# VectorE's queue in a neighbourhood-quantile stage: from the planner's order to one written out by hand

## The chip, the cores and the metric

The kernel runs on one core of a Trainium2 chip. The metric is the device time in microseconds (us) of one launch, as the median of several runs. Each engine of a core (TensorE, VectorE, ScalarE, GpSimd, SyncE; in the profile PE, DVE, ACT, POOL, SP) works through a queue of its own in order. An instruction that waits for a semaphore holds up all that stand behind it on its engine.

## The reference

Sixteen graphs of 1024 nodes with 64 channels go through four layers, each followed by a residual sum and a layer norm. Layers 0, 1 and 3 are a normalised propagation, a gated 8-head attention and a plain propagation. Layer 2 is the one that matters here. Its core is this:

```python
nd = adj_d > 0                                   # some neighbours are thinned out first
s = jnp.sort(jnp.where(nd[..., None], x[:, None, :, :], jnp.inf), axis=2)
nv = nd.sum(2)
for tau, w in zip((0.25, 0.5, 0.75), (0.25, 0.5, 0.25)):
    pos = tau * jnp.maximum(nv - 1, 0)
    lo, hi = floor(pos), ceil(pos)
    agg = agg + w * (v_lo + (pos - lo) * (v_hi - v_lo))   # v_lo = s[..., lo, :], v_hi = s[..., hi, :]
```

For every node and channel it takes three quantiles over the node's neighbours, each interpolated between two order statistics. A two-layer network follows.

## The kernel before

The kernel handles two graphs at a time, in eight passes. A pass has layer 0, then attention (during which the sorting network for the previous pair runs on VectorE), then the quantile stage of the previous pair (`quantiles`). Layers 2 and 3 of a pair end one pass later.

No neighbour list is sorted in the quantile stage. Each channel's 1024 values were sorted once over all nodes, and a node's neighbour set is a bit pattern over the sorted order: 32 words of 32 bits. The stage finds the word that holds the wanted order statistic, takes that word out, finds the bit in it, and looks the value up:

- `words` makes E, 0/1 and power-of-two matrices, on VectorE (an "E-word", two instructions of 128x1024). `half_word` multiplies E with the neighbour matrix on TensorE (one magic matmul and eight of 128x512), and ScalarE evicts the result into V (three 16-bit planes: a running count and the two halves of the word).
- A *step* is one (group of four channels, quantile) pair. 16 groups x 3 quantiles x 2 graphs give 96 steps; eight steps make a *unit*, so there are twelve units.
- `compare` (L900, VectorE, 128x2048) compares the running counts with the limits: `lt`. `one_hot` takes differences of neighbouring rows by four matmuls with `dif`, and ScalarE casts them into `oh`, which marks the word.
- `pick` (L918, VectorE, two instructions of 128x3072) multiplies V by the one-hots: `m`, two buffers. `sum_words` (12 small matmuls, `tonesb`) adds the rows up into `wps`, one PSUM tile per unit.
- After the eighth step of a unit, `kth_bit` searches all of the unit's words for the bit: one ScalarE cast of wps to `wb`, then about fifty short VectorE instructions on 16-bit integers, in five parts between `yield`s, giving `r2` and `r64`.
- `distances` (12 matmuls with `pen`, 16 with `bd`), `least_values` (4) and `sum_values` (8, f32) then look the value up, one earlier step (`look`) at a time, and the last of a unit multiplies by the weights and writes the result out (L983, L984).

The PSUM banks of `bank` are four, shared by half words, one-hots and distances.

Who orders what: TensorE's instructions in the stage go through `product`, which ties each to the one before it, so their order is that of the program. All other engines are ordered by the framework's planner, which puts an instruction that it expects to be ready ahead of one that it expects to wait. In program order a step is: pick (two products), compare for the next step, distances, half of the half words, least values, one-hot of the next step, sum of values, the other half words, `sum_words`, a part of the search in steps 0 to 3, and new E-words in steps 4 to 7. `MORE` says how many half words a step has. Lookups trail the products by 8 + `PARTS` = 12 steps. After step 96 a tail does the last twelve lookups.

Of the kernel before, what the change touches and what calls it, by code (L numbers as in the profile page):

```python
# [25 lines left out]
P = 128  # L26
# [8 lines left out]
OFF = 8192.0  # L35
OFF0 = 128.0
# [6 lines left out]
PARTS = 4  # L43
LAG = PARTS + 1
MORE = (1, 3, 3, 3, 1, 0, 0, 0)
# [75 lines left out]
def gnn_kernel(ctx: ExitStack, tc: tile.TileContext, a: dict, out: bass.AP):  # L121
# [558 lines left out]
    def rank_limits(gr, qe, qn):  # L680
# [14 lines left out]
        def limits(q):  # L695

            lim = gr.lim[q] = qe.tile([P, 2, N], U16, name="lim", bufs=LB)
            nc.scalar.activation(lim[:, 0], cnt, AF.Copy, scale=0.25 * (q + 1), bias=-0.25 * (q + 1) - 0.375)
            for s in (1, 0):
                nc.vector.tensor_scalar(lim[:, s], lim[:, 0], 32.0, OFF0 + 32.0 * (s + 1), op0=ALU.mult, op1=ALU.add)  # L700

# [21 lines left out]
    def kth_bit(pool, wps, kd, r2, r64):  # L723


        sh = [P, 512]
        v = nc.vector

        def u16(name, shape=sh):
            return pool.tile(shape, U16, name=name)  # L730

        wb = pool.tile([P, NW, 512], BF, name="wb")
        nc.scalar.copy(wb, wps)
        yield
        X = wb.bitcast(U16)
        v.tensor_scalar(X[:, 0], X[:, 0], OFF0, None, op0=ALU.subtract)
        v.tensor_scalar(X[:, 1:3], X[:, 1:3], OFF, None, op0=ALU.subtract)
        k = u16("k")
        S = u16("S", [P, 2, 512])
        U = u16("U", [P, 2, 512])  # L740
        a, c = U[:, 0], S[:, 0]
        v.tensor_scalar(a, X[:, 0], 5, None, op0=ALU.logical_shift_right)
        v.tensor_tensor(k, kd, a, ALU.subtract)
        v.tensor_scalar(X[:, 0], X[:, 0], 31, None, op0=ALU.bitwise_and)

        def counts(x, s1, s2, s4, t):

            v.tensor_scalar(t, x, 1, 0x5555, op0=ALU.logical_shift_right, op1=ALU.bitwise_and)
            v.tensor_tensor(s1, x, t, ALU.subtract)
            v.tensor_scalar(t, s1, 2, 0x3333, op0=ALU.logical_shift_right, op1=ALU.bitwise_and)  # L750
            v.tensor_scalar(s2, s1, 0x3333, None, op0=ALU.bitwise_and)
            v.tensor_tensor(s2, s2, t, ALU.add)
            v.tensor_scalar(t, s2, 4, None, op0=ALU.logical_shift_right)
            v.tensor_tensor(s4, s2, t, ALU.add)
            v.tensor_scalar(s4, s4, 0x0F0F, None, op0=ALU.bitwise_and)

        counts(X[:, 0:2], S, S, S, U)
        yield
        v.tensor_scalar(U, S, 8, None, op0=ALU.logical_shift_right)
        v.tensor_tensor(S, S, U, ALU.add)  # L760
        v.tensor_scalar(S, S, 0x1F, None, op0=ALU.bitwise_and)

        M = u16("M", [P, 2, 512])
        v.tensor_tensor(a, S[:, 0], S[:, 1], ALU.add)
        v.tensor_tensor(M[:, 0], S[:, 0], k, ALU.is_le)
        v.tensor_tensor(M[:, 1], a, k, ALU.is_le)
        v.tensor_tensor(S, S, M, ALU.mult)
        v.tensor_tensor(k, k, S[:, 0], ALU.subtract)
        v.tensor_tensor(k, k, S[:, 1], ALU.subtract)
        v.copy_predicated(X[:, 0], M[:, 0], X[:, 1])  # L770
        v.copy_predicated(X[:, 0], M[:, 1], X[:, 2])
        pos = u16("pos")
        v.tensor_scalar(pos, M[:, 0], 5.0, None, op0=ALU.mult)
        v.tensor_scalar(a, M[:, 1], 14.0, None, op0=ALU.mult)
        v.tensor_tensor(pos, pos, a, ALU.add)
        yield

        counts(X[:, 0], X[:, 1], X[:, 2], c, a)
        for width, z, mask in ((8, None, 15), (4, 2, 15), (2, 1, 3), (1, 0, 1)):
            v.tensor_scalar(c, c if z is None else X[:, z], mask, None, op0=ALU.bitwise_and)  # L780
            v.tensor_tensor(a, c, k, ALU.is_le)
            if width > 1:
                v.tensor_tensor(c, c, a, ALU.mult)
                v.tensor_tensor(k, k, c, ALU.subtract)
                v.tensor_scalar(a, a, float(width), None, op0=ALU.mult)
                n = {8: 3, 4: 2, 2: 1}[width]
                v.tensor_tensor(X[:, 0:n], X[:, 0:n], a[:, None, :].to_broadcast([P, n, 512]),  # L787
                                ALU.logical_shift_right)
            v.tensor_tensor(pos, pos, a, ALU.add)
            if width == 8:  # L790
                yield
        v.tensor_scalar(r64, pos, 64.0, None, op0=ALU.mult)
        searched[:] = [v.tensor_tensor(r2, pos, pos, ALU.mult)]  # L793

    def words(pool, g, w, rk, u_w, b_w):
# [12 lines left out]
        if w == 0:  # L808
            d = Ev.bitcast(F16)
            nc.vector.tensor_tensor(d, over_j(tk_c), over_t(u_w), ALU.subtract)  # L810
            nc.vector.tensor_scalar(Ev, d, 0.0, 2048.0, op0=ALU.max, op1=ALU.min)
        else:
            nc.vector.tensor_tensor(Ev, over_t(rk), over_j(t_c), ALU.is_equal)
            nc.vector.tensor_tensor(Ev, Ev, over_t(b_w), ALU.mult)
        return E

    def quantiles(ip, rk, u_w, b_w):
# [12 lines left out]
        with ExitStack() as es:  # L830

            kb, qe, qn = [es.enter_context(tc.tile_pool(name=name, bufs=1, reuse_waits="tile"))
                          for name in ("kb", "qe", "qn")]
# [43 lines left out]
            def half_word(gr, g, w, hf, matmul):  # L877
# [10 lines left out]
                if w == 0:  # L888
                    nc.scalar.activation(gr.V[g][:, 0, cols], ps, AF.Copy, scale=2.0 ** -6,  # L889
                                         bias=OFF0 - MAGIC[0] / 64 - 63 / 128)  # L890
# [6 lines left out]
            def compare(u, s):  # L897
                gr, g, q = u.pairs[s]
                u.lt = qe.tile([P, 2, N], BF, name="lt", bufs=LTB)
                nc.vector.tensor_tensor(u.lt, gr.V[g][:, None, 0, :].to_broadcast([P, 2, N]), gr.lim[q], ALU.is_lt)  # L900

            def one_hot(u, s):
                oh = qn.tile([P, 2, N], F16, name="oh", bufs=U8N + LAG)
                for kk in range(2):
                    for hf in range(2):
                        cols = slice(hf * 512, (hf + 1) * 512)
                        ps = bank([P, 512])
                        product(ps, dif, u.lt[:, kk, cols], start=True, stop=True)
# [3 lines left out]
            def pick(u, s):  # L912
                gr, g, q = u.pairs[s]
                u.m = [None, None]
                nonlocal picked
                for kk in range(2):
                    u.m[kk] = qe.tile([P, NW, N], BF, name="m", bufs=2)
                    picked = nc.vector.tensor_tensor(u.m[kk], gr.V[g].bitcast(BF),  # L918
                                            u.oh[s][:, kk, None, :].to_broadcast([P, NW, N]), ALU.mult)

            def sum_words(u, s):
                if s == 0:
                    u.wps = psw.tile([P, NW, 512], F32, name="wps")
                for w in range(NW):
                    for t in (1, 3, 0, 2):
                        hf, kk = t // 2, t % 2
                        product(u.wps[32 * t:32 * t + 32, w, :], tonesb[:, s, :],
                                u.m[kk][:, w, hf * 512:(hf + 1) * 512],
# [5 lines left out]
            def distances(u, s, spare=False):  # L934
# [13 lines left out]
                if spare:  # L948
                    for h in range(2):
                        x = qn.tile([P, 2, N], F16, name="oh", bufs=U8N + LAG)  # L950
# [21 lines left out]
            def sum_values(u, s):  # L972
# [4 lines left out]
                if s == U8N - 1:  # L977
                    res = qn.tile([P, 512], F32, name="vals", bufs=5)
                    if u is units[-1]:
                        nc.scalar.copy(res, u.acc)  # L980
                        nc.gpsimd.tensor_tensor(res, res, gr.cf[u.n % 3], ALU.mult)
                    else:
                        nc.vector.tensor_tensor(res, u.acc, gr.cf[u.n % 3], ALU.mult)  # L983
                    nc.gpsimd.dma_start(agg_d[gr.bb][:, u.n, :], res)  # L984
# [4 lines left out]
            units = [SimpleNamespace(n=i // U8N % NU, pairs=pairs[i:i + U8N], oh=[], vals={}) for i in range(0, len(pairs), U8N)]  # L989
# [6 lines left out]
            def elements():  # L996
# [4 lines left out]
                gr.E.setdefault(g, []).append(words(qe, gr.bb * G + g, w, rk, u_w, b_w))  # L1001
                made += 1

            def more_elements():
                while todo and made + 1 <= used // 2 + EB:
                    elements()

            def more_words(n, matmul=product):
                nonlocal used
                for k, w, hf in islice(halves, n):  # L1010
                    while len(groups[k][0].E.get(groups[k][1], [])) <= w:
                        elements()
# [4 lines left out]
            with tc.high_priority():  # L1017
                while made < 2 * EW:
                    elements()
            more_words(2 * EW, nc.tensor.matmul)  # L1020
            more_elements()
# [7 lines left out]
            compare(*steps[0])  # L1029
            one_hot(*steps[0])  # L1030
# [3 lines left out]
            search = None  # L1034
            for i, (u, s) in enumerate(steps):
# [17 lines left out]
                pick(u, s)  # L1053
                if i + 1 < len(steps):
                    compare(*steps[i + 1])
                if look:
                    distances(*look)
                more_words(more // 2)
                if look:
                    least_values(*look)  # L1060
                if i + 1 < len(steps):
                    one_hot(*steps[i + 1])
                if look:
                    sum_values(*look)
                more_words(more - more // 2)
                sum_words(u, s)
                if s < PARTS and search is not None:
                    next(search, None)
                if s >= PARTS or i < U8N:
                    more_elements()  # L1070
                if s == U8N - 1:
                    u.r2 = qn.tile([P, 512], F16, name="r2", bufs=2)
                    u.r64 = qn.tile([P, 512], F16, name="r64", bufs=2)
                    search = kth_bit(kb, u.wps, u.pairs[0][0].kc[u.n % 3], u.r2, u.r64)
                    next(search)
            before = None
            for i, look in enumerate(steps[-U8N - PARTS:]):
                if i < PARTS:
                    next(search, None)
                if before and i == PARTS:  # L1080
                    sum_values(*before)
                    before = None
                distances(*look, spare=i % 2 == 1)
# [4 lines left out]
            sum_values(*before)  # L1088

# [255 lines left out]
```

## Time and profile before

| | us |
|---|---|
| median of 3 runs (12822.29 to 12823.69) | 12823.57 |
| the profiled execution | 12824.17 |
| its span, first to last instruction | 12822.4 |
| VectorE busy, whole span | 10529.5 |
| TensorE busy, whole span | 11097.9 |
| ScalarE busy, whole span | 7375.6 |
| products L918, 1536 of 1753 ns | 2636.8 |
| compares L900, 768 of 1220 ns | 936.8 |

A group's row gives the busy time, the mean of one in ns, the idle time of its engine just ahead of it, and what ended that. A matmul's end is modelled, so TensorE's busy share is an upper bound of its work; what it could do is better read from distances between starts.

From the timeline, the first product of the first stage starts at 1262.4 and the last one ends at 2110.6: 848.2 us for 96 steps. From first product to first product the twelve units of that stage take 56.0, 76.7, 70.1, 75.0, 75.4, 74.7, 70.3, 70.2, 71.2, 70.3, 70.2 and 68.3 us. The tail's last lookup ends 60.9 us after the last product. The other seven stages agree with this within 2.5 us in each unit.

### The profile page before, as it was taken

Reading aid. Unit: us, or ns where it says so; the run is one execution under the profiler, and the core shown is the slowest. Engines: PE = TensorE matmul, PEld = TensorE weight load, DVE = VectorE, ACT = ScalarE, POOL = GpSimd, SP = SyncE. Lnnn points to the kernel's source line nnn. Section 1 sums busy time; section 2 is a strip of 40 time slices with the busy share of each in tenths; the row PEclk is TensorE's granted clock in tenths of the full one; section 3 lists DMA queues with packets and bytes.
Section 4 is the critical chain, followed back from the end, with each engine's and each line's share of the span. In section 5 each row is a group of like instructions: output and inputs, shape, how many; then the busy total and the mean of one; then the engine's idle time right before and its main releaser. Section 6 shows DMA issues by size and latency. Waiting matters only on the chain.

```text
span 12822.4 us, 208955 instructions
## 1 busy us (share of the span) xinstructions
PE 11097.9 (87%) x82560; PEld 4623.9 (36%) x82560; DVE 10529.5 (82%) x18662; ACT 7375.6 (58%) x13684; POOL 547.1 (4%) x836
## 2 busy tenths in 40 slices
PE   7989897998979899798997989879898798983897
PEld 3545222552225422254222532235322353221222
DVE  3587898788977889788996889968898788988895
ACT  4656565565646566465664656646566465651564
POOL 0000000000000000000000000000000000000000
PEclk8989998999989999899998999989899899996998
DMA  2021002200031000310003100031000410002001
GB/s 81 31 90 39 4 5 97 65 26 4 6 103 62 23 5 5 121 46 20 5 6 125 44 18 5 6 128 42 16 5 6 135 44 8 8 14 88 4 5 47
DMA packets 352246, 510.07 MB, mean 40 GB/s; under 512 B 120480, under 2 KB 275488, under 8 KB 349216
## 3 DMA queue, kind: packets, MB, share of 16 engines
q1 hardware_dynamic: 288656, 367.77, 8.8%
q10 hardware_dynamic: 33040, 86.88, 2.0%
q0 software_dynamic: 29568, 42.05, 1.1%
q8 instruction: 649, 10.63, 0.3%
q14 instruction: 333, 2.73, 0.1%
HBM read 380.08 MB, written 116.46 MB: 39 GB/s over the span
## 4 chain that ended last, share of the span: by engine, by line
PE 49%; DVE 25%; ACT 13%; issue 4%; DMA 4%; SPq 0%; ACTq 0%; DVEq 0%
PE bank L875 18%; ACT vals L961 7%; PE banks L536 6%; PE bank L558 5%; PE bank L572 5%; DVE m L918 5%; PE acc L875 4%; PE wps L875 2%; DVE key L1184 2%; PE bank L412 2%; DMA at<-in_adjT 2%; PE banks L387 1%; DVE lt L900 1%; DVE s L543 1%; DVE wb L787 1%
## 5 line engine op out<-in xcount | busy, mean ns | idle before, releaser
L918 DVE TENSOR_TENSOR m<-V,oh 128x3072 bf16<-128x3072 bf16 x1536 | 2636.8, 1753 | 274.8 <-PE wps L875 228.1
L961 ACT ACTIVATE vals<-bank 128x512 f32<-128x512 f32 x2880 | 1488.1, 602 | 1382.2 <-PE bank L875 1381.1
L875 PE MATMUL bank<-ndT,E 128*128 128x512 fp8e4 x7936 | 1914.9, 385 | 0.0
L543 DVE CUSTOM_DVE_ANT_0 s<-banks,adj 128x1024 f32<-128x1024 f32 x1024 | 1214.8, 1221 | 643.9 <-PE banks L536 639.6
L909 ACT CAST oh<-bank 128x512 f16<-128x512 f32 x3072 | 1595.2, 632 | 94.3 <-PE bank L875 94.1
L875 PE MATMUL bank<-lt,dif 128*128 128x512 bf16 x3072 | 1073.5, 393 | 319.7 <-DVE lt L900 73.1
L562 ACT COPY pT<-bank 128x512 f32<-128x512 f32 x1536 | 802.4, 594 | 815.3 <-PE bank L558 815.3
L551 ACT ACTIVATE s<-s,mx 128x1024 f32<-128x1024 f32 x1024 | 1176.4, 1160 | 73.6 <-DVE mx L543 71.0
L536 PE MATMUL banks<-kT,qT 64*128 64x512 f32 x4096 | 1115.3, 626 | 63.6 <-DVE mx L543 40.6
L900 DVE TENSOR_TENSOR lt<-V,lim 128x2048 bf16<-128x2048 uint16 x768 | 936.8, 1220 | 228.6 <-PE bank L875 228.3
L875 PEld LDWEIGHTS <-E 128*128 128x128 bf16 x7936 | 701.6, 98 | 1055.8 <-issue 367.8
L558 PEld LDWEIGHTS bank<-ident,s 128*128 128x128 f32 x8192 | 897.1, 142 | 405.5 <-issue 288.7
L558 PE MATMUL bank<-ident,s 128*128 128x128 f32 x8192 | 1028.9, 280 | 0.0
L572 PE MATMUL bank<-pT,v 128*64 128x256 f32 x8192 | 1007.8, 389 | 0.0
L875 PE MATMUL bank<-r,pen 32*128 32x512 f16 x5856 | 614.0, 391 | 418.4 <-DVE r L793 368.5
L875 PE MATMUL bank<-oh,bd 64*64 64x512 f16 x11712 | 818.5, 393 | 0.0
L875 PE MATMUL acc<-vals,bonesf 128*32 128x512 f32 x5760 | 794.3, 616 | 0.0
L875 PE MATMUL wps<-m,tonesb 128*32 128x512 bf16 x9216 | 656.2, 387 | 71.7 <-DVE m L918 71.7
L889 ACT ACTIVATE V<-bank 128x512 uint16<-128x512 f32 x512 | 305.6, 597 | 657.7 <-PE bank L875 601.4
L893 ACT ACTIVATE V<-bank 128x512 uint16<-128x512 f32 x512 | 306.0, 598 | 641.6 <-PE bank L875 631.3
L572 PEld LDWEIGHTS bank<-pT,v 128*64 128x64 f32 x8192 | 548.5, 138 | 313.9 <-issue 50.9
L1184 DVE TENSOR_TENSOR key<-key 128x512 f32<-128x512 f32 x880 | 579.2, 688 | 26.4 <-DMA key<-x2T_d 25.5
(274 smaller groups left out, 14426.5 us busy)
## 6 DMA issues: line engine op xcount, KB each, us to landing
at<-in_adjT SPq DMA_DIRECT2D x256, 512.0 KB, 5.6
masks_d<-mask SPq DMA_DIRECT2D x440, 128.0 KB, 1.7
mask<-masks_d SPq DMA_DIRECT2D x440, 128.0 KB, 2.1
adj<-in_adj SPq DMA_DIRECT2D x96, 512.0 KB, 5.3
ad<-in_adj ACTq DMA_DIRECT2D x64, 512.0 KB, 6.2
agg_d<-vals POOLq DMA_DIRECT2D x96, 256.0 KB, 2.3
agg<-agg_d ACTq DMA_DIRECT2D x16, 1536.0 KB, 8.6
nd_d<-nd SPq DMA_DIRECT2D x128, 128.0 KB, 1.9
```

The source lines that it names most:

```text
L536: then(nc.tensor.matmul(ss[h][:, hf * 512:(hf + 1) * 512], gr.qk[hp, 0][HALF[h], k * P:(k + 1) * P], gr.qk[hp, 1][HALF[h], hf * 512:(hf + ...
L543: last = nc.vector.tensor_tensor_reduce(s, ss[h], gr.adj[k], -1.0, 3.0e38, ALU.add, ALU.min, mx)
L551: then_act(nc.scalar.activation(s, s, AF.Exp, bias=mx, scale=-1.0, accum_out=sm))
L558: then(nc.tensor.transpose(ps[:, m, :], exps[h][0][:, (4 * mh + m) * P:(4 * mh + m + 1) * P], ident))
L562: then_act(nc.scalar.copy(dst, ps))
L572: then(nc.tensor.matmul(po[HALF[h]], gr.v[:, 4 * mh + m, (2 * hp + h) * C:(2 * hp + h + 1) * C], pT[h][mh][:, m, :], start=(mh == 0 and m ...
L875: then(nc.tensor.matmul(*args, **kw))
L900: nc.vector.tensor_tensor(u.lt, gr.V[g][:, None, 0, :].to_broadcast([P, 2, N]), gr.lim[q], ALU.is_lt)
L909: nc.scalar.copy(oh[:, kk, cols], ps)
L918: picked = nc.vector.tensor_tensor(u.m[kk], gr.V[g].bitcast(BF), u.oh[s][:, kk, None, :].to_broadcast([P, NW, N]), ALU.mult)
L961: nc.scalar.activation(vals[t], ys[t], AF.Relu)
L1184: i = v.tensor_tensor(*args)
```

## The change

- VectorE's instructions of the stage that go through a new helper `InOrder` (products, compares, E-words, the search, the result's multiply) are tied to each other in program order, as TensorE's are.
- The search is cut into 27 *runs*, and its instructions are rearranged so that a run ends where the next instruction needs the last one's result. `RUNS` says how many runs a step has, in six steps instead of four. They alternate with the large instructions of the step: product, run, (result, run,) product, run, compare, run, halves of E-words and runs.
- Compares and one-hots are made two steps ahead, and two of each are made before the loop. `lt` and `m` move to a pool of their own; their buffer counts stay 1 and 2.
- In TensorE's order the least values come right after the distances, then one half word, the one-hot, a further half word where `MORE` is 2, the sum of values, `sum_words`.
- The offsets of the three planes of V become equal (256), so one ScalarE pass removes them from `wb` instead of two VectorE subtractions. Some masks in the bit counts are left out or moved.
- `PARTS` is 6: lookups trail by 14 steps. The result's multiply and its DMA come one step later. At most `AT_ONCE` E-words are made in a step.

```diff
+RUNS = (5, 4, 2, 8, 3, 5)
+PARTS = len(RUNS)
+AT_ONCE = (1, 1, 0, 1, 0, 1, 2, 2)
+MORE = (1, 2, 1, 2, 1, 2, 1, 1)
-PARTS = 4
-MORE = (1, 3, 3, 3, 1, 0, 0, 0)
...
+    class InOrder:
+        def __init__(self):
+            self.then = in_sequence()
+        def __getattr__(self, name):
+            def op(*args, **kw):
+                i = getattr(nc.vector, name)(*args, **kw)
+                self.then(i)
+                return i
+            return op
...
         nc.scalar.copy(wb, wps)
+        nc.scalar.activation(X, X, AF.Copy, bias=-OFF)
         yield
-        X = wb.bitcast(U16)
-        v.tensor_scalar(X[:, 0], X[:, 0], OFF0, None, op0=ALU.subtract)
-        v.tensor_scalar(X[:, 1:3], X[:, 1:3], OFF, None, op0=ALU.subtract)
         v.tensor_scalar(a, X[:, 0], 5, None, op0=ALU.logical_shift_right)
+        v.tensor_scalar(X[:, 0], X[:, 0], 31, None, op0=ALU.bitwise_and)
         v.tensor_tensor(k, kd, a, ALU.subtract)
-        v.tensor_scalar(X[:, 0], X[:, 0], 31, None, op0=ALU.bitwise_and)
...
+        def nibbles(x, s1, s2, s4, t):
             v.tensor_scalar(t, x, 1, 0x5555, op0=ALU.logical_shift_right, op1=ALU.bitwise_and)
+            yield
             v.tensor_tensor(s1, x, t, ALU.subtract)
+            yield
             v.tensor_scalar(t, s1, 2, 0x3333, op0=ALU.logical_shift_right, op1=ALU.bitwise_and)
             v.tensor_scalar(s2, s1, 0x3333, None, op0=ALU.bitwise_and)
+            yield
             v.tensor_tensor(s2, s2, t, ALU.add)
+            yield
             v.tensor_scalar(t, s2, 4, None, op0=ALU.logical_shift_right)
+            yield
             v.tensor_tensor(s4, s2, t, ALU.add)
-            v.tensor_scalar(s4, s4, 0x0F0F, None, op0=ALU.bitwise_and)
+            yield
+        yield from nibbles(X[:, 0:2], S, S, S, U)
+        v.tensor_scalar(U, S, 8, 15, op0=ALU.logical_shift_right, op1=ALU.bitwise_and)
+        v.tensor_scalar(S, S, 15, None, op0=ALU.bitwise_and)
+        yield
         v.tensor_tensor(S, S, U, ALU.add)
-        v.tensor_scalar(S, S, 0x1F, None, op0=ALU.bitwise_and)
+        yield
         v.tensor_tensor(a, S[:, 0], S[:, 1], ALU.add)
         v.tensor_tensor(M[:, 0], S[:, 0], k, ALU.is_le)
         v.tensor_tensor(M[:, 1], a, k, ALU.is_le)
+        yield
+        v.copy_predicated(X[:, 0], M[:, 0], X[:, 1])
         v.tensor_tensor(S, S, M, ALU.mult)
+        v.tensor_scalar(pos, M[:, 0], 5.0, None, op0=ALU.mult)
         v.tensor_tensor(k, k, S[:, 0], ALU.subtract)
+        yield
+        v.tensor_scalar(a, M[:, 1], 14.0, None, op0=ALU.mult)
         v.tensor_tensor(k, k, S[:, 1], ALU.subtract)
         v.copy_predicated(X[:, 0], M[:, 1], X[:, 2])
         v.tensor_tensor(pos, pos, a, ALU.add)
+        yield from nibbles(X[:, 0], X[:, 1], X[:, 2], c, a)
+        v.tensor_scalar(c, c, 15, None, op0=ALU.bitwise_and)
+        for width, z, mask in ((8, 2, 15), (4, 1, 3), (2, 0, 1)):
+            yield
             v.tensor_tensor(a, c, k, ALU.is_le)
+            yield
+            v.tensor_tensor(c, c, a, ALU.mult)
+            v.tensor_scalar(a, a, float(width), None, op0=ALU.mult)
+            v.tensor_tensor(k, k, c, ALU.subtract)
+            n = z + 1
+            v.tensor_tensor(X[:, 0:n], X[:, 0:n], a[:, None, :].to_broadcast([P, n, 512]),
+                            ALU.logical_shift_right)
             if width == 8:
                 yield
+            v.tensor_tensor(pos, pos, a, ALU.add)
+            v.tensor_scalar(c, X[:, z], mask, None, op0=ALU.bitwise_and)
+        yield
+        v.tensor_tensor(a, c, k, ALU.is_le)
+        yield
+        v.tensor_tensor(pos, pos, a, ALU.add)
+        yield
         v.tensor_scalar(r64, pos, 64.0, None, op0=ALU.mult)
         searched[:] = [v.tensor_tensor(r2, pos, pos, ALU.mult)]
...
-                u.lt = qe.tile([P, 2, N], BF, name="lt", bufs=LTB)
+                u.lt[s] = qm.tile([P, 2, N], BF, name="lt", bufs=LTB)
...
-                oh = qn.tile([P, 2, N], F16, name="oh", bufs=U8N + LAG)
+                oh = qn.tile([P, 2, N], F16, name="oh", bufs=U8N + PARTS + 2)
...
-            compare(*steps[0])
-            one_hot(*steps[0])
+            for st in steps[0:2]:
+                compare(*st)
+                one_hot(*st)
...
-                pick(u, s)
-                if i + 1 < len(steps):
-                    compare(*steps[i + 1])
+                def large():
+                    pick(u, s, 0)
+                    yield
+                    if results:
+                        result()
+                        yield
+                    pick(u, s, 1)
+                    yield
+                    if i + 2 < len(steps):
+                        compare(*steps[i + 2])
+                        yield
+                    yield from more_elements(AT_ONCE[s] if i >= U8N else 2)
+                for _ in zip_longest(large(), islice(search, RUNS[s] if s < PARTS else 0)):
+                    pass
                 if look:
                     distances(*look)
+                    least_values(*look)
+                more_words((more + 1) // 2)
+                if i + 2 < len(steps):
+                    one_hot(*steps[i + 2])
                 more_words(more // 2)
                 if look:
-                    least_values(*look)
-                if i + 1 < len(steps):
-                    one_hot(*steps[i + 1])
-                if look:
                     sum_values(*look)
-                more_words(more - more // 2)
                 sum_words(u, s)
-                if s < PARTS and search is not None:
-                    next(search, None)
-                if s >= PARTS or i < U8N:
-                    more_elements()
```

## Prediction

> **What bounds the kernel now.** I read the page first, then the stage windows. The quantile stage runs eight times, some 910 us each, so it is over half of the span.
>
> ```profile
> PE 11097.9 (87%) x82560; PEld 4623.9 (36%) x82560; DVE 10529.5 (82%) x18662; ACT 7375.6 (58%) x13684; POOL 547.1 (4%) x836
> ```
>
> In the windows (PE, PEld, DVE, ACT and POOL busy) the first row is one stage, the second one unit of eight steps inside it:
>
> ```profile
> 1235.00:2145.00 910.00, 794.58 (x6296) 250.11 (x6300) 817.86 (x1231) 547.10 (x1036) 47.98 (x86) 0.95 0.03 9
> 1760.50:1830.70 70.20, 66.71 (x551) 20.91 (x547) 66.18 (x100) 45.39 (x88) 4.85 (x9) 1.00 0.02 6
> ```
>
> TensorE and VectorE are both 95% busy in a unit, so neither can be late without the unit growing. The list of waits shows how they hold each other, over all eight stages (us, times, longest):
>
> ```profile
> PE bank L875 <- DVE r L793: 368.5, 56, 18.3
> ...
> DVE lt L900 <- PE bank L875: 228.3, 255, 5.9
> DVE m L918 <- PE wps L875: 228.1, 304, 2.9
> ```
>
> The timeline of the end of a unit, with no search in it, shows one step in full:
>
> ```profile
> 1748.45 0.83 PE L875 MATMUL wps<-m,tonesb 128*32 128x512 bf16 x12
> 1749.22 0.61 PE L875 MATMUL bank<-r,pen 32*128 32x512 f16 x8
> 1749.38 3.43 DVE L918 TENSOR_TENSOR m<-V,oh 128x3072 bf16<-128x3072 bf16 x2 [0.47 <-PE wps L875]
> ...
> 1751.36 1.84 PE L875 MATMUL bank<-lt,dif 128*128 128x512 bf16 x4
> ...
> 1753.13 1.06 PE L875 MATMUL acc<-vals,bonesf 128*32 128x512 f32 x8
> 1753.24 1.23 DVE L900 TENSOR_TENSOR lt<-V,lim 128x2048 bf16<-128x2048 uint16 x1 [0.43 <-PE bank L875]
> 1754.02 0.83 PE L875 MATMUL wps<-m,tonesb 128*32 128x512 bf16 x12
> ```
>
> Two things matter. The products (m, L918) wait until the sums (wps) of the step before have read the only two m buffers: the sums end at 1749.28, the products start at 1749.38. And the planner put the compare for one-hot j+1 ahead of the products of step j, so its one-hot (1751.36) had lt long before, and only the products stood before the sums. TensorE's queue is full: 5.56 us per step (1748.45 to 1754.02) plus 2.14 for each half word (1740.35 to 1742.49), 10.67 of them per unit: 8 x 5.56 + 10.67 x 2.14 = 67.3, of 70.3.
>
> **What the change does to this loop.** TensorE's written order in step i is now: lookup, half word, one-hot i+2, perhaps another half word, sum of values, sums i. VectorE's is: product, run, product, run, compare i+2, and the rest. So the one-hot needs the compare that stands *behind* this step's products, the sums stand behind the one-hot in one queue, and the next products need the sums. That is a closed loop through both engines. What is queued behind the waiting product on VectorE is everything: its order is fixed, so search and E-words cannot pass. The old waits on lt and m go; this one is next late. Step by step:
>
> - Two products start 1.68 apart (3.43 - 1.75) and the compare takes 1.22: 2 x 1.68 + 1.22 = 4.58.
> - The runs between them. An instruction followed by an independent one costs its duration less some 0.09: 128x512 scalar ops 0.20, tensor ops 0.34; 128x1024 0.34 and 0.60; predicated copies 0.60; shifts 0.87, 0.61 and 0.34. The two runs ahead of the compare come, for s = 0 to 5, to 1.68, 1.28, 3.42, 0.74, 0.88, 2.10; in s = 6 the result multiply (0.68, L983) costs 0.61; in s = 7 nothing. Together 10.7.
> - From the compare's end: 0.06 to the one-hot; four one-hot matmuls 1.07 with free banks (1295.54 to 1296.61), 1.20 behind a half word (1715.27 to 1716.47), 1.77 as above, waiting for banks; I take 1.15, since a half word now gives the banks time; 0.88 (1753.13 to 1754.02, sum of values), 0.83 (sums), 0.09 to the product: 3.01. A half word behind the one-hot makes it 5.15, in s = 1, 3, 5 (s = 3 in two units of three).
> - VectorE's work behind the compare hides inside this: 0 us in s = 2, 2.0 in s = 4, 2 to 3 elsewhere. Only in s = 3 is it about 4.7 (runs of 0.34, 0.20, 0.34, 0.20, 0.34 and 1.75, 0.4 for dependent neighbours, an E-word of 1.1), above the 3.01 of every third unit.
> - TensorE's work in front of the one-hot (1.74 + 0.40 + 2.14 = 4.3) lies beside products and compare, and so sets nothing.
> - First run of a unit: wps goes through a ScalarE cast (1.44, L733) and now a second ScalarE pass in place of two VectorE subtractions (0.29 + 0.42). No row shows it; its nearest are 1.05 (128x1024, L698) and the cast's 1.44 on as many elements. I take 1.44. The run is ready 3.1 us after the sums, the product ahead of it ends after 1.84: 1.3 of wait in s = 0 (0 if ScalarE is quicker, 4 if four evictions go between).
>
> So the steps are 10.6, 11.0, 11.0, 10.3, 8.5, 11.8, 8.2, 7.6: **79.0 us per unit**, where today's are 70.3 (units 2 and 6 to 10) and 75 (3 to 5, which also prepare the second graph).
>
> **What is saved** lies beside this loop. VectorE loses the two subtractions and two masks (0.42 + 0.29; a third only changes place): 1.4 us a unit. Neighbours that depend on each other are split:
>
> ```profile
> 1719.17 0.43 DVE L781 TENSOR_TENSOR U<-S,k 128x512 uint16<-128x512 uint16 x1
> 1719.63 0.42 DVE L783 TENSOR_TENSOR S<-S,U 128x512 uint16<-128x512 uint16 x1
> 1720.09 0.43 DVE L784 TENSOR_TENSOR k<-k,S 128x512 uint16<-128x512 uint16 x1
> 1720.43 0.29 DVE L785 TENSOR_SCALAR U<-U 128x512 uint16<-128x512 uint16 x1
> ```
>
> Dependent ones start 0.03 after the last ended, independent ones 0.09 before: 0.12 a pair, some 30 pairs, 3.6 us a unit. VectorE's own work would then be near 62 us of 79, so none of it reaches the end. [...]
>
> **The sum**, per stage. Units 2 to 10: 9 x 79.0 = 711, plus half of the 14 us of second-graph work (the rest falls into the new waits): 718 against 647, +71. Unit 0 has neither lookup nor search: 8 x (4.58 + 2.13) + 3 x 2.14 = 60.1 against 56.0, +4. Unit 1 has no lookup until s = 6, so no sum of values: 79.0 - 6 x 0.88 + 0.5 (s = 3 is then set by VectorE's 4.7) = 74.2 against 76.8, -3, as its 18.3 us wait for the first search goes: lookups now trail by 14 steps, not 12. Unit 11 runs out of half words after s = 1 and has no compare in the last two steps (9.0 in s = 3, 9.7 in s = 5, 5.0 and 3.4 at the end): 68 against 68, 0. Tail: the two extra lookups fill the 12.2 us that TensorE waits there for the last search; -2. The result DMA moves one step later past POOL's bd loads; nobody reads it before the stage ends, so 0. Together +71, times 8 = +567. The profiled execution took 12824.17 (span 12822.4); with the median of 12823.57 it comes to 12,824 + 567 = **13,390 us**.
>
> **Rivals.**
> 1. *Faster.* The loop is slack, because the work behind each compare covers TensorE's answer. It decides where that work exceeds 3.0 (5.2) us in every step. TensorE alone would then set the unit: 67.3 less 8 x 0.6 of bank waits = 62.4, with some loss 66. 9 units save 4.2 each, the second graph's 14 us and 9 of unit 1 go: -61 x 8, about 12,340. For it: the runs are nearly equal, 2.9 to 3.9 us a step. Against it: 10.7 of their 20 us stand ahead of the compare, and s = 2 keeps none behind it. 0.12.
> 2. *No difference.* The loop binds but at 70 us: it would need the answer in 1.9 instead of 3.0, which the rows exclude, or a VectorE order in which only neighbours through the new helper are tied and the planner still lifts compares. About 12,820. 0.02.
> 3. *Slower still.* The first run waits 4 us, not 1.3, and one-hots stay at 1.77: 2.7 + 5.0 per unit, +77 a stage, near 14,000; half of it, 13,700. TensorE also slows after long idling (r,pen 1.04 instead of 0.61 after the 18.3 us wait); I assume 1 to 3 us do not. 0.16.
> 4. *My forecast*, +42 (no first-run wait, one-hot 1.07, second graph free) to +100 a stage (a third of case 3's +77 more): 13,160 to 13,620. 0.70.
>
> Range 13,050 to 13,760: cases 4 and half of 3, with the low end stretched towards 1. A measurement tells 0.2% (26 us) from no change: faster 0.12, same 0.02, slower 0.86.
>
> **What would show it.** Right: products waiting on wps with over 1,000 us in the waits; one-hots waiting on lt in nearly every step; lt no longer waiting on the bank; VectorE and TensorE each near 62 to 66 us of a 79 us unit; step s = 2 near 11 us with nothing between compare and product; r waits short. Wrong: a unit at or under 70 us, or VectorE over 90% busy in it.

## The result, and the profile after

The changed kernel takes **13,796.67 us** (median of 4 runs, 13,784.33 to 13,805.12) beside 12,822.93 for the kernel before (12,809.88 to 12,823.69): 1.076 times as long, interval 1.0743 to 1.0780. I had said 13,390 and a range of 13,050 to 13,760. The direction and the loop are as predicted; 975 us were lost (span 12,822.4 to 13,797.8) where I had 567.

The page's first part, of after:

```profile
PE 11133.8 (81%) x82560; PEld 4686.0 (34%) x82560; DVE 10347.7 (75%) x18278; ACT 7564.9 (55%) x13780; POOL 541.8 (4%) x836
```

VectorE has 182 us less to do, TensorE about what it had, and both now stand still more. In the windows (PE, PEld, DVE, ACT and POOL busy, then the granted clock) the first row is one stage, the second one unit of eight steps:

```profile
1263.00:2230.00 967.00, 752.23 (x5913) 240.28 (x5913) 747.23 (x1078) 535.36 (x988) 39.88 (x74) 0.92 0.02 4
1861.00:1943.00 82.00, 66.19 (x551) 21.47 (x547) 65.30 (x97) 47.44 (x88) 4.84 (x9) 0.94 0.02 5
```

The unit of 70.2 us has become one of 82.0, with the same 66 us of TensorE and 65 of VectorE in it. The list of waits (us, times, longest) says what fills the rest:

```profile
DVE m L732 <- PE wps L901: 1550.4, 708, 5.3
PE bank L901 <- DVE lt L732: 1511.5, 736, 6.3
...
DVE U L732 <- ACT wb L754: 147.7, 96, 4.7
```

(Every instruction that goes through the new in-order helper has line 732, every matmul that goes through `product` line 901.) There are 768 steps in the kernel. In 708 of them VectorE's product waits for the sums, and in 736 TensorE's one-hot waits for the compare: the two engines wait for each other in turn. VectorE's timeline shows one turn, step s = 2:

```profile
1934.21 1.75 DVE L732 TENSOR_TENSOR m<-V,oh 128x3072 bf16<-128x3072 bf16 x1
...
1937.47 0.29 DVE L732 TENSOR_SCALAR U<-wb 128x512 uint16<-128x512 uint16 x1
1937.68 1.22 DVE L732 TENSOR_TENSOR lt<-V,lim 128x2048 bf16<-128x2048 uint16 x1
1944.10 1.76 DVE L732 TENSOR_TENSOR m<-V,oh 128x3072 bf16<-128x3072 bf16 x1 [5.19 <-PE wps L901]
1945.77 0.42 DVE L732 TENSOR_TENSOR wb<-wb,U 128x512 uint16<-128x512 uint16 x1
```

After the compare nothing is queued ahead of the next product, so VectorE stands for 5.19 us until that may begin. The search instruction behind it had its operands at 1937.76 (1937.47 + 0.29) and starts at 1945.77, in its place in the queue. TensorE's timeline shows what it does in that time, and the same chain one step later:

```profile
1938.96 1.89 PE L901 MATMUL bank<-lt,dif 128*128 128x512 bf16 x4 [3.99 <-DVE lt L732]
1940.78 1.94 PE L901 MATMUL acc<-vals,bonesf 128*32 128x512 f32 x8
1942.48 1.51 PE L901 MATMUL wps<-m,tonesb 128*32 128x512 bf16 x12
...
1949.46 1.04 PE L901 MATMUL bank<-lt,dif 128*128 128x512 bf16 x4 [1.16 <-ACT V L917]
1950.42 1.06 PE L901 MATMUL acc<-vals,bonesf 128*32 128x512 f32 x8
1951.31 0.83 PE L901 MATMUL wps<-m,tonesb 128*32 128x512 bf16 x12
```

After 3.99 us of idleness the same 24 matmuls take 1938.96 to 1943.99, 5.03 us; after 1.16 us they take 2.68. The windows around them give the granted clock (the last column but two):

```profile
1935.00:1938.90 3.90, 0.00 (x0) 0.00 (x0) 3.87 (x7) 1.09 (x2) 0.00 (x0) 0.78 0.00 2
1938.90:1944.00 5.10, 5.04 (x28) 1.23 (x32) 0.00 (x1) 2.05 (x4) 0.00 (x0) 0.50 0.00 0
1944.00:1949.40 5.40, 4.30 (x41) 1.42 (x41) 5.30 (x7) 3.13 (x6) 0.00 (x0) 1.00 0.00 0
```

The clock is halved for the whole stretch in which VectorE waits for TensorE. That is the part that I had left out. In these rows it is back at full rate some 5 us after the work starts, but it fell before the work did start: a mean of 0.78 over 3.90 us leaves 1.7 us at half rate, so it fell near 1937.2, some 2.2 us after TensorE's last matmul (1938.96 - 3.99 = 1934.97). In this trace the clock has two levels, 1.00 and 0.50, and changes only on a grid of 3.41 us. Two stretches of that grid show the fall:

```profile
1933.82:1937.24 3.42, 1.15 (x6) 0.30 (x4) 3.42 (x7) 1.45 (x3) 0.00 (x0) 1.00 0.01 2
1937.24:1940.65 3.41, 1.69 (x4) 0.43 (x4) 1.63 (x3) 1.05 (x3) 0.00 (x0) 0.50 0.00 0
```

In the first TensorE still works for 1.15 of 3.42 us, a third, and in the next the clock is at half. Between the first and last product of the eight stages of after it falls 266 times, each time behind a stretch of 3.41 us in which TensorE was busy for 56% or less (median 34%). The 1,655 stretches behind which it stayed at full rate were busy for 41% or more. At 144 of the 266 falls no single wait that reaches into the stretch was as long as it, 3.41 us.

### The profile page after: what moved, and what is told of

It reads as the page before. It is cut to its first block, busy times and chain, and to the rows that moved or that the text cites. A ratio compares the mean times of both kernels' runs of the same rounds, so it can differ in the third digit from the quotient of the medians.

```text
span 13797.8 us, 207830 instructions
## 1 busy us (share of the span) xinstructions
PE 11133.8 (81%) x82560; PEld 4686.0 (34%) x82560; DVE 10347.7 (75%) x18278; ACT 7564.9 (55%) x13780; POOL 541.8 (4%) x836
## 4 chain that ended last, share of the span: by engine, by line
PE 50%; DVE 33%; ACT 5%; issue 5%; DMA 3%; POOL 0%; DVEq 0%; ACTq 0%; SPq 0%; POOLq 0%
PE bank L901 16%; DVE m L732 11%; PE acc L901 6%; DVE lt L732 6%; PE banks L536 5%; PE bank L558 5%; PE bank L572 5%; PE wps L901 5%; DVE S L732 3%; DVE U L732 2%; DVE wb L732 2%; DMA at<-in_adjT 2%; PE bank L412 2%; DVE key L1239 1%; PE banks L387 1%
## 5 line engine op out<-in xcount | busy, mean ns | idle before, releaser
L732 DVE TENSOR_TENSOR m<-V,oh 128x3072 bf16<-128x3072 bf16 x1536 | 2682.4, 1755 | 1583.2 <-PE wps L901 1550.4
L901 PE MATMUL bank<-lt,dif 128*128 128x512 bf16 x3072 | 910.2, 416 | 1562.3 <-DVE lt L732 1511.5
L901 PE MATMUL bank<-ndT,E 128*128 128x512 fp8e4 x7936 | 2009.0, 399 | 0.0
L543 DVE CUSTOM_DVE_ANT_0 s<-banks,adj 128x1024 f32<-128x1024 f32 x1024 | 1214.8, 1221 | 633.7 <-PE banks L536 627.8
L901 PEld LDWEIGHTS <-dif 128*128 128x128 bf16 x3072 | 251.0, 101 | 2109.1 <-DVE lt L732 1883.6
L901 PE MATMUL acc<-vals,bonesf 128*32 128x512 f32 x5696 | 912.6, 704 | 0.0
L901 PE MATMUL wps<-m,tonesb 128*32 128x512 bf16 x9216 | 765.1, 438 | 0.0
L536 PEld LDWEIGHTS banks<-kT,qT 64*128 64x128 f32 x4096 | 400.9, 190 | 537.6 <-issue 349.9
```

Source lines behind the costliest of these rows:

```text
L536: then(nc.tensor.matmul(ss[h][:, hf * 512:(hf + 1) * 512], gr.qk[hp, 0][HALF[h], k * P:(k + 1) * P], gr.qk[hp, 1][HALF[h], hf * 512:(hf + ...
L543: last = nc.vector.tensor_tensor_reduce(s, ss[h], gr.adj[k], -1.0, 3.0e38, ALU.add, ALU.min, mx)
L732: i = getattr(nc.vector, name)(*args, **kw)
L901: then(nc.tensor.matmul(*args, **kw))
```

## Experiments

Two theories stood at the start. **Order**: the compare behind the products closes a loop through both queues, and its place alone makes the kernel slow. **Contents**: the new arithmetic, the second ScalarE pass, the search cut into small pieces or the two-step lead cost time of their own. A third question is why the loss is 975 and not 567.

"Main" below is the time from the start of a stage's first product to the end of its last, a mean of the eight stages: 849.0 before, 965.7 after. Units and steps are timed from first product to first product.

### The compare ahead of the two products

```diff
 def large():
+    if i + 2 < len(steps):
+        compare(*steps[i + 2])
     pick(u, s, 0)
...
     pick(u, s, 1)
     yield
-    if i + 2 < len(steps):
-        compare(*steps[i + 2])
-        yield
```

> Changed kernel, with the compare of step i+2 put ahead of the two products of step i in VectorE's fixed order; TensorE's order is as in the changed kernel. Theory (closed loop): what matters is on which side of the products the compare stands; one-hots find lt ready, their waits on lt fall from 1511 us to under 300, units to 66 to 70 us, the time to 12,450 to 12,850 us. Rival (two steps ahead or a fixed order is bad in itself): over 13,500 us.

Measured: 12,576.01 us, 0.9809 (0.9794 to 0.9824) of the kernel before, 1,221 us less than after. Main is 811.2. Its waits, and its windows of one stage and one unit:

```profile
DVE lt L732 <- PE bank L901: 228.5, 144, 2.9
DVE m L732 <- PE wps L901: 143.5, 218, 3.0
DVE U L732 <- ACT wb L754: 134.0, 88, 4.7
PE wps L901 <- DVE m L732: 114.7, 90, 4.0
```

```profile
1263.00:2074.00 811.00, 700.74 (x5902) 240.01 (x5905) 746.17 (x1078) 527.46 (x985) 40.15 (x74) 0.98 0.02 5
1735.50:1804.80 69.30, 62.04 (x551) 21.53 (x547) 65.03 (x97) 46.80 (x88) 4.83 (x9) 1.00 0.02 6
```

The instructions are the same, VectorE is as busy as in after (746 of 811 us, not of 967), and the two long waits have gone. Here is its VectorE and TensorE in a step:

```profile
1761.05 1.22 DVE L732 TENSOR_TENSOR lt<-V,lim 128x2048 bf16<-128x2048 uint16 x1
...
1762.18 1.75 DVE L732 TENSOR_TENSOR m<-V,oh 128x3072 bf16<-128x3072 bf16 x1
...
1764.19 1.75 DVE L732 TENSOR_TENSOR m<-V,oh 128x3072 bf16<-128x3072 bf16 x1
...
1765.65 0.81 PE L901 MATMUL bank<-lt,dif 128*128 128x512 bf16 x3
```

The compare ends at 1762.27; its one-hot starts 3.38 us later, when TensorE gets to it, and waits for nothing. The time and the waits are as expected. So one place in one queue makes the difference between the change's loss and a gain of 247 us.

### The one-hot behind the sums

This opens the loop on the other engine.

```diff
-if i + 2 < len(steps):
-    one_hot(*steps[i + 2])
 more_words(more // 2)
 if look:
     sum_values(*look)
 sum_words(u, s)
+if i + 2 < len(steps):
+    one_hot(*steps[i + 2])
```

> Changed kernel, with one_hot moved behind sum_words in TensorE's order; all else stays. Theory (closed loop: the sums stand behind a one-hot whose compare stands behind this step's products): the loop is open, the products wait for sums that wait for nothing but the products before them. Units fall from 82 us to TensorE's own 67 to 70, the waits of products on wps from 1550 us to under 400, the time to 12,550 to 12,900 us. Rival (the fixed VectorE order, or the added ScalarE pass, costs by itself wherever the one-hot stands): units stay over 78, the time over 13,500 us.

Measured: 13,052.25 us, 1.0179 (1.0162 to 1.0196). It takes back 744 of the 974 us and misses its range of 12,550 to 12,900.

```profile
DVE m L732 <- PE wps L901: 713.4, 481, 5.5
DVE U L732 <- ACT wb L754: 295.4, 96, 4.7
```

The one-hot's four banks now come right before the four of the distances, which wait for ScalarE to empty banks: the eight `r,pen` matmuls take 2.06 us instead of 0.61. And the sums' casts queue behind the one-hot's, so the first run waits 2.9 us a unit ((295.4 - 37.6) / 88; the 37.6 are eight waits of 4.7 behind the last units). Opening a loop moves what follows it: the new order met the banks. That these two make up the whole miss is not shown.

### No search between the products or ahead of the compare

```diff
     pick(u, s, 0)
-    yield
     if results:
         result()
-        yield
     pick(u, s, 1)
-    yield
     if i + 2 < len(steps):
         compare(*steps[i + 2])
```

> Changed kernel, with no search run between the two products or ahead of the compare: products, result, compare, then runs and E-words in turn. Theory (the runs ahead of the compare lengthen the loop by 10.7 us a unit, and waits over 2.5 us make the next matmuls slow): both go, units near 69 to 72 us (4.58 + the larger of 2.8 or 5.0 and 3 to 5.4 us of runs, per step), the time 12,800 to 13,050 us. Rival (the runs are small, the compare behind the products is all): 13,600 us and over.

Measured: 12,835.29 us, 1.0010 (1.0000 to 1.0019); main 846.7. The loop is still there, with 676.2 us of products waiting and 680.0 of one-hots, but the work that was ahead of the compare now lies behind it, beside TensorE's answer. Units 2 to 10 are 10.7 us shorter each (646.8 us together, not 743.2), as much as those runs take. The equality is partly luck, because the clock changed with them: it is at half rate for 450 us of the eight stages, not 1,162. The run shows that work ahead of the compare is in the loop, and not its price alone.

### One step ahead instead of two

```diff
-for st in steps[0:2]:
+for st in steps[0:1]:
...
-        compare(*steps[i + 2])
+        compare(*steps[i + 1])
...
-    one_hot(*steps[i + 2])
+    one_hot(*steps[i + 1])
```

> Changed kernel with compares and one-hots made one step ahead, in the same places of both queues. Theory (the place of the compare relative to the products closes the loop, by how many steps it is ahead does not matter): the same loop, 13,600 to 14,000 us, products still waiting on wps for over 1,300 us. Rival (one-hots made a step earlier are what puts them in the way of the sums): under 13,200 us.

Measured: 13,853.56 us, 1.0808 (1.0793 to 1.0823), with 1,610.7 us of m waits. That is 57 us beyond after. The lead buys next to nothing while TensorE's own order puts the early one-hot ahead of this step's sums.

### The planner's order for VectorE

```diff
-v = InOrder()
+v = nc.vector
```

> Changed kernel with the helper that ties VectorE's instructions taken out: same program order, same TensorE order, same arithmetic, but the planner orders VectorE again. Theory (the tied order closes the loop, as it keeps the compare behind the products): the planner lifts compares ahead of waiting products, one-hot waits on lt fall from 1511 us to under 500, the time to 12,450 to 12,900 us. Rival (TensorE's new order, two steps ahead or lookups 14 steps behind cost by themselves): over 13,300 us.

Measured: 12,789.83 us, 0.9974 (0.9964 to 0.9984).

```profile
PE bank L901 <- DVE lt L926: 209.0, 120, 4.0
...
DVE m L942 <- PE wps L901: 105.0, 203, 1.8
```

The time and the waits are as expected. With everything else of the change in place and only VectorE's order left to the planner, compares are lifted ahead of products again. The contents of the change are therefore not what costs 974 us; VectorE's written order is.

### The new arithmetic alone

To the kernel before: the cast and a second ScalarE pass in place of the two subtractions, one offset of 256 for all words, and two masks fewer (the cut shows one of the mask lines).

```diff
+nc.scalar.copy(wb, wps)
+nc.scalar.activation(X, X, AF.Copy, bias=-OFF)
-v.tensor_scalar(X[:, 0], X[:, 0], OFF0, None, op0=ALU.subtract)
-v.tensor_scalar(X[:, 1:3], X[:, 1:3], OFF, None, op0=ALU.subtract)
...
-    v.tensor_scalar(s4, s4, 0x0F0F, None, op0=ALU.bitwise_and)
```

> The kernel before with only the changed search arithmetic: equal offsets taken off by a second ScalarE pass, masks left out. Order, steps ahead and lookups as before. Theory (TensorE's queue sets the unit before, VectorE's saved 1.4 us lies mostly beside it): 0 to 60 us less, 12,760 to 12,824 us. Rival (VectorE bounds the unit): 1.4 us x 96 units = 135 us less, 12,690 us or under. Rival (the second ScalarE pass is in the way): over 12,850 us.

Measured: 12,849.59 us, 1.0019 (1.0010 to 1.0028). I had expected 0 to 60 us less. Taking 1.4 us of VectorE a unit away gains nothing, and with the second ScalarE pass in its place the kernel is 27 us longer; units 2 to 10 take 653.6 us instead of 647.0. A VectorE that alone bounds the unit would have gained. What costs the 27 us stays open: the only waits of VectorE for the second pass are the eight behind the last units (38.0 us in all), and a later start of the first run as the cause was not tried.

### The waits filled with matmuls

The question of size. TensorE runs matmuls that nobody reads ahead of the one-hot, about as long as its wait there; VectorE's order is that of after.

```diff
+n = {0: 8, 1: 5, 2: 14, 5: 10}.get(s, 0) + (0 if look else 8)
+if n and i + 2 < len(steps):
+    ps = bank([P, 512])
+    for _ in range(n):
+        product(ps, dif, graphs[0].ndT[:, 0, 0:512], start=True, stop=True)
 if i + 2 < len(steps):
     one_hot(*steps[i + 2])
```

> Changed kernel, with added matmuls of 128x512 that nobody reads ahead of the one-hot in the steps where TensorE waits longest for the compare (8, 5, 14, 10 in steps 0, 1, 2, 5 of a unit, 8 more where there is no lookup yet). Theory (some 45 to 60 us of each stage are matmuls that run at about half rate after a wait of 2.5 us or more): the loop stays, products still wait on wps for over 1,200 us, but the chain from one-hot to sums is back to 2.7 or 4.9 us everywhere, and the time falls to 13,300 to 13,500 us although TensorE does more. Rival (the extra over the predicted 79 us a unit is from ScalarE's second pass or from VectorE): the time stays at 13,800 us or grows.

Measured: 13,521.88 us, 1.0545 (1.0529 to 1.0560). The added group, and the product's wait:

```profile
L901 PE MATMUL bank<-ndT,dif 128*128 128x512 fp8e4 x4448 | 1033.5, 380 | 0.0
```

```profile
DVE m L732 <- PE wps L901: 1314.4, 695, 5.2
```

TensorE does 1,033.5 us more and the kernel ends 275 us *earlier*: the mean granted clock goes from 0.918 to 0.949, and within the stages it is at half rate for 273 us instead of 1,162. The time ends 22 us above the range expected. In units 2 to 10 the steps s = 0 to 7 now take 10.55, 11.03, 10.95, 10.37, 8.28, 11.84, 8.26 and 7.41 us (medians), and the nine units together 716.4 us. My prediction had 10.6, 11.0, 11.0, 10.3, 8.5, 11.8, 8.2, 7.6 and 718. In after the medians are 11.72, 11.03, 12.59, 10.38, 8.28, 13.35, 8.26 and 7.41, and the units 743.2. So the loop is as I drew it, on a TensorE that is hardly slowed, and all that came on top in these units sits in the steps 0, 2 and 5, where the filling is (step 1 is filled too, and equal). Units 0 and 11 do not come back: 66.8 and 73.0 us, 6.7 and 5.0 above my terms. Why was not tried.

### Going on from the compare in front

Three variants of the best kernel. The first (the compare in front, and in s = 0 both products ahead of the first run) asks whether the first-run wait costs anything:

```diff
     pick(u, s, 0)
-    yield
+    if s:
+        yield
```

> The kernel with the compare ahead of the products, and in the first step of a unit also both products ahead of the first search run. Theory (that run waits 1.4 us per unit for ScalarE's two passes over wb, 134 us in all, with the second product behind it): the wait goes, the first step falls from 9.8 to some 8.5 us, the time by 90 to 150 us to 12,430 to 12,490 us. Rival (TensorE or ScalarE sets that step): the wait goes and the time stays within 30 us of 12,576.

Measured: 12,572.60 us, 0.9810 (0.9796 to 0.9823), no different from 12,576, as the rival had it. The wait has gone from every unit but the last of each stage (37.6 us are left of 134.0); the median of step 0 fell from 9.8 to 8.9 us and that of step 1 rose from 8.9 to 9.8. The two steps together take as long as before, so it was not VectorE's wait that set them.

The second also takes the result multiply of the last unit but one from VectorE:

```diff
-if u is units[-1]:
+if u is units[-1] or u is units[-2]:
     nc.scalar.copy(res, u.acc)
```

> The kernel with the compare ahead of the products, and the result of the last unit but one multiplied by ScalarE and GpSimd, as that of the last unit is, and not by VectorE. Theory (in the tail of seven stages that multiply stands in VectorE's queue behind the search and behind instructions of the next sort, and the first lookup of the last unit waits 5 to 12 us for its accumulator): tails shorten from 68 to about 60 us, the time by 40 to 70 us to 12,505 to 12,535 us. Rival (the next pass starts beside the tail, so its length is hidden): within 15 us of 12,576.

Measured: **12,562.72 us**, 0.9791 (0.9778 to 0.9804), the lowest median of all. In the seven stages that it concerns, the time from the last product to the last lookup matmul fell from some 68 us (74 in the seventh) to 61 to 62.5, as meant, but little of the 40 to 70 us arrived: 13 us between the medians, 23 by the two ratios, whose intervals overlap. That the rest lies beside the next stage's work is argued.

The third puts all runs of that kernel behind the second product:

```diff
     pick(u, s, 0)
-    yield
     if results:
         result()
-        yield
     pick(u, s, 1)
     yield
```

> As the last, and all search runs behind the second product: compare, product, product, then runs and E-words in turn. Theory (with the compare ahead TensorE's queue sets the unit, 5.56 us a step and 2.14 a half word, 67.3 us; the runs between the products delay the sums only where TensorE has nothing else): waits of the sums on m fall, units go from 69.4 to 68 to 69 us, the time by 0 to 120 us to 12,400 to 12,530. Rival (splitting dependent neighbours pays, VectorE bounds the unit): runs that meet each other cost 0.12 us a pair, the time is 30 to 100 us longer than with runs between.

Measured: 12,591.12 us, 0.9811 (0.9797 to 0.9824), 28 us more than without the edit, where I had expected 0 to 120 less; main 816.4 instead of 810.6. Having search runs between the products is worth some 6 us a stage, once the order is right. How much of it is the splitting of dependent neighbours, and how much the place of the runs, this does not tell. Products wait for sums 345 times here and 222 times there.

## Why the prediction was right in direction and short in size

1. **The closed loop: right.** Over 1,000 us of m waits (1,550.4), one-hots waiting on lt in nearly every step (736 of 768), nothing between compare and product in s = 2, and both engines at 65 to 66 us of a unit were the marks that I had named. The compare in front removes the loop; it shows the cause.
2. **The two runs ahead of the compare: right.** With TensorE kept at work the eight steps have medians within some 0.2 us of my numbers, and these hold the runs. Taking the runs out of the loop brings main from 965.7 to 846.7, but part of that is the clock.
3. **The first-run wait of 1.3 us: right.** (147.7 - 37.6) / 88 = 1.25 us a unit; the second ScalarE pass took 1.48.
4. **TensorE's answer: the step that failed.** "I assume 1 to 3 us do not" slow TensorE. I priced the chain from the first one-hot matmul to the end of the sums at 2.86 us, with a half word in it at 5.0, whatever wait stood before it. That is the term that was too small.
   - After waits of 0.5 to 1.5 us the medians are 2.68 and 4.91, as priced. After 3.5 to 4.0 us (66 cases) the first is 4.31, never under 3.81. After 2 to 3 us it goes either way: 45 chains without a half word and 29 with one run at full clock and take 2.68 and 4.91, and 49 and 34 run at half clock for more than 0.5 us and take 3.78 to 5.03 and 6.42 to 6.59.
   - Over all 752 chains, what was measured less what I had comes to 45.6 us a stage. (A chain without the sum of values is taken as 0.88 shorter.) Main is 965.7 where my terms make 718 + 60.1 + 74.2 + 68 = 920.3, so 45.4 are missing. The two agree by units as well: 4.3 and 5.3 us in unit 0, 8.1 and 8.4 in unit 1, 27.4 and 25.2 in units 2 to 10, 5.9 and 6.4 in unit 11.
   - With the waits filled that excess is 3.7 us a stage, and units 2 to 10 are back at 716.4 of my 718. There the cause is shown. For the 20 us of units 0, 1 and 11 it rests on the agreement alone, as filling brought back only unit 1 (82.6 to 76.5).
   - I had seen the 1.04 us beside 0.61 for one group after a long wait, and put it into the rival "slower still" alone. The trace of the kernel before already spoke against "1 to 3 us": in its stages the clock falls 65 times, and at 31 of these no wait that reaches into the stretch of 3.41 us before it was 3 us long.
5. **The tail: wrong in sign.** I had -2 us a stage; it went from 60.5 to 67.9. The wait for r did shrink (368.5 us to 25.4). But the result multiply now stands in VectorE's written order behind the search, and the planner puts the next stage's sort ahead of it. The timeline of a stage's end:

```profile
2258.82 1.04 PE L901 MATMUL bank<-r,pen 32*128 32x512 f16 x8 [4.22 <-DVE r L732]
...
2263.75 2.62 DVE L1239 TENSOR_TENSOR key<-key 128x512 f32<-128x512 f32 x4
...
2266.28 0.69 DVE L732 TENSOR_TENSOR vals<-acc,cf 128x512 f32<-128x512 f32 x1
...
2267.02 0.62 PE L901 MATMUL acc<-oh,base 128*32 128x512 f16 x4 [4.89 <-DVE vals L732]
```

   TensorE waits 4.9 us here, up to 12.2 in other stages, for an accumulator that a 0.69 us multiply would free. The last stage, with no sort behind it, has 59.3. I had listed the result's DMA as moved, and not the multiply as one whose reader is TensorE. The variant that moves it off VectorE (on the kernel with the compare in front) shows the cause, some 68 to 61 to 62.5, and also that little of it reaches the time.
6. **What adds up.** 8 x (45.4 + 9.4) = 438 us over my sum, of which 975 - 567 = 408 show in the time. The other 30 should lie beside work of the neighbouring stages; that is argued, not shown.
7. **The rivals.** "Loop is slack" and "no difference" fell with the 1,550 us of waits. "Slower still" had the right sign, and 13,797 lies in its range of 13,700 to 14,000 by luck: it priced a first run that waits 4 us and one-hots of 1.77, and the first run waited 1.25. Of its grounds only the slowed TensorE was there, and that it had set aside for short waits.

## What to carry to other kernels

Where two in-order queues feed each other, write down for each step which instruction waits for the other engine and what must already stand in front of it: whatever the other engine needs next has to be queued ahead of one's own waiting instruction. Making something "two steps ahead" doesn't help when it stands behind the wait; the same instructions took 13,797 us with the compare last and 12,576 with it first. And when a sum makes TensorE wait some microseconds in every step, price the work after the wait at the slowed rate that the trace shows for such a place (here 4.31 us), not at the rate of the busy loop (2.68); here the share of work in a stretch of 3.41 us (a median of 34% ahead of the 266 falls) told more than the length of one wait (at 144 of them none was that long).

## What was unexpected in the hardware

- TensorE was slow after some waits of 2 to 3 us and not after others. The same 24 matmuls took 2.68 us after 0.5 to 1.5 us of idleness, 4.31 after 3.5 to 4.0, and after 2 to 3 us either 2.68 (45 cases) or 3.78 to 5.03 (49 cases), as the clock stayed or fell. At 144 of the 266 falls of the clock no wait that reaches into the 3.41 us before was that long. What goes with the falls is the share of work: they follow stretches of 3.41 us that are busy for 56% or less. Stretches of 41 to 56% are found on both sides, and the matmuls' ends are modelled, so the bound is no sharper than that. It is read from the clock records; no run varied the share alone.
- With more to do TensorE ran faster here: 4,448 unread matmuls (1,033.5 us) took the mean granted clock from 0.918 to 0.949 and brought the whole kernel 275 us forward.
